# Layer 1: delta-x transposes of two groups right after delta x, first sum of y of each group one step on, 432 tokens of the C products on VectorE

## The chip, the cores and the metric

The kernel runs on one core of one Trainium2 chip. The metric is the device time of one execution in microseconds (us); the time before is the median of three runs. A profile of one execution shows the engines: PE (TensorE matmul; PEld is its weight load), DVE (VectorE), ACT (ScalarE), POOL (GpSimd) and SP (SyncE, which issues the DMAs).

## The reference

A batch of 32 images of 96 channels and 56x56 pixels goes through two layers. Layer 0 is an inverted-residual convolution block (1x1, depthwise 3x3, squeeze-excite, 1x1). Layer 1, which the change concerns, is two Mamba blocks in a row over the 3136 tokens of each image, then a 1x1 fusion and a batch norm. Cut to what matters, one Mamba block is:

```python
h  = layernorm(seq);  xs, z = split(h @ in_w)          # 96 -> 2 x 192
xc = silu(causal_conv4(xs) + conv_b)
dt, Bm, Cm = split(xc @ xproj_w)                        # 6, 16, 16
delta = softplus(dt @ dt_w + dt_b)                      # 192 channels
dA  = exp(delta[..., None] * A)                         # 192 x 16 states a token
dBx = delta[..., None] * Bm[:, :, None, :] * xc[..., None]
hstates = scan over tokens: h = dA * h + dBx
y   = einsum('blds,bls->bld', hstates, Cm) + Dp * xc
out = seq + (y * silu(z)) @ out_w
```

All arithmetic is float32.

## The kernel before, in words

Layer 1 works in chunks of 784 tokens: 32 images of 4 chunks, each through two blocks, so 256 chunks ("units" in the code). The chunks of the two blocks alternate. A chunk takes 24 steps, one scan each. There are three groups (k = 0, 1, 2) of 64 channels, and a group has eight steps in four pairs (j = 0 to 3, four of the 16 states each). A scan works on 128 partitions, 32 channels times four states, over 784 tokens.

What one step needs, with the names and lines that the profile uses:

- `da` (L1004, ACT): exp(delta * A). In the pair j = 0 of a group it goes to a lent buffer in SBUF, shown as `bx<-deltab`; in all other steps to a PSUM tile of the pool `dpool`, which has two buffers.
- `bx` (L1041, POOL): delta x times B, for a pair of steps at once, in the pairs j = 1 to 3.
- `bp` (L1018, PE, in `fill`): the same product for the pair j = 0, made by matmuls from `ut`, the transposed delta x of the group, and `diag`, a block-diagonal of B. It goes to a buffer of the same `dpool`, so the bp of step t can't begin before the scan of step t-2 is done. In a chunk these are steps 0, 1, 8, 9, 16 and 17; `fill(at + 1)` stands in the program one step ahead of its scan.
- `hh` (L1052, DVE): the scan itself.
- `hc`: hh times C for a pair of steps. The first LP tokens of each step are DVE's (L1060), from `cp`, a copy of C in PSUM that ACT makes (L1029); the other tokens are POOL's (L1068).
- `y`: ACT seeds the PSUM tile of a group with Dp * xc (L1086, `seed`); PE adds the sum over states of each pair to it (L1099, `reduce`); DVE multiplies the finished y by the gate z (L1110, `gated`). There is one PSUM buffer for y, so the seed of a group waits for the gate product of the group before.
- `state` (L1077, ACT): the last column of a pair's scans, kept for the next chunk of the image.

Between these stands the preparation of later chunks, a list of (time, function) pairs written out by hand in `prepare`. Time is counted in steps; step 0 is two chunks before the chunk's own first scan, so that its own steps are 48 to 71, and the steps 24 to 47 fall together with the 24 steps of the chunk before. Within a step the fraction sets the place: below 0.05 ahead of the step's seed and exp; 0.05 to 0.08 after bp and ahead of the sums of y; all others at the end. The functions that matter here, at the places in the chunk that is being scanned:

- step 2 to 5: `conv`, PE's matmuls of xs (L773) for the chunk after next, and `keep` copies them out as xc (L784, ACT); they use the banks of pool `pp`, two buffers which all small PE results share in the order in which they are asked for;
- steps 9 to 12: the output projection `o` (L905, L909), the gate projection `z` (L789) and the centering of a later chunk, `cen` (L702), whose squares ACT takes as `sx` (L707);
- step 14: `variance` (L712, var), 14 PE rows from both halves of sx; step 17: the root on ACT and three small Newton instructions on DVE (L729 to L734);
- steps 9 to 11: `input_u` (L864, POOL) makes delta x (`us`) of the three groups for the next chunk;
- `turn_u` (L848, PE) transposes the us of one group into a bank, and `keep_u` (L854 and L855, ACT) copies it to `ut`. Group 0 does this in steps 19 and 20 of the chunk before; groups 1 and 2 in steps 5 to 7 of their own chunk;
- step 7: the Softplus burst on ACT, and step 15 the Silu burst: a change of the activation table, one or two passes and a change back.

The order on each engine is that of the program (`tc.manual_schedule()`); only the semaphore waits decide when an instruction starts. The body of a step is in this order: inject, early preparation, seed, decay, bring, bursts, scan, gated, product, save, rest, fill, preparation from 0.05 to 0.08, reduce, preparation from 0.08, fetch (the DMAs).

Of the kernel before, what the change touches and what calls it, by code (L numbers as in the profile page):

```python
# [24 lines left out]
NL, NS, DIN, RANK, KC = 2, 16, 192, 6, 4  # L25
LC = 784
HB = LC // 2
LP = 416
NQ = L // LC
RB = HB // W  # L30
DG = 8
# [29 lines left out]
def conv_mamba_kernel(ctx, tc, a, out):  # L61
# [43 lines left out]
    with ExitStack() as ph:  # L105
# [119 lines left out]
        for i in range(NHB):  # L225
            t = hp3.tile([128, H + 2, W + 2], F32, name=f"hpad{i}", tag=f"hpad{i}")
# [303 lines left out]
    with ExitStack() as ph:  # L530
# [14 lines left out]
        def bank(name):  # L545
            return pp.tile([128, 512], F32, name=name, tag="p")

        def wt(shape, tag, bufs, n):
            return work.tile(shape, F32, name=f"{tag}_{n}", tag=tag, bufs=bufs)
# [132 lines left out]
        def cols(h):  # L682
            return slice(h * HB, h * HB + HB)

        def prepare(n):
# [14 lines left out]
            def center(h):  # L700
                ps = d["cen", h] = bank(f"cen_{n}_{h}")
                pe.matmul(ps[:C, :HB], cen, seqs[c, i][:, cols(h)], start=True, stop=True)  # L702

            def square(h):
                if h == 0:
                    d["sq"] = wt([128, LC], "sx", 1, n)[:C]
                s.activation(d["sq"][:, cols(h)], d["cen", h][:C, :HB], AF.Square)  # L707
# [17 lines left out]
            def newton(step):  # L725
                va, rs = d["va"], d["rs"]
                if step == 0:
                    d["nw"] = wt([TK, NK], "nw", 1, n)
                    v.scalar_tensor_tensor(d["nw"], rs, -0.5, va, ALU.mult, ALU.mult)  # L729
                if step == 1:  # L730
                    v.tensor_mul(d["nw"], d["nw"], rs)
                if step == 2:
                    to = wt([TK, NK], "rs", 1, n)
                    v.scalar_tensor_tensor(to, d["nw"], 1.5, rs, ALU.add, ALU.mult)  # L734
                    d["rs"] = to
                    if q == 0:
                        g.memset(xn[:, : KC - 1], 0.0)
# [40 lines left out]
            def keep(tag, bufs, ps, k):  # L778
                if k == 0:
                    d[tag] = wt([128, NB, HB], tag, bufs, n)  # L780
                if tag == "dl":
                    s.activation(d[tag][:, k, :], d[ps, k][:, :HB], AF.Identity, bias=dp[:, i, k, 0:1])
                else:
                    s.copy(d[tag][:, k, :], d[ps, k][:, :HB])  # L784
# [22 lines left out]
            def project_dt(k):  # L807
                ps = d["dtp", k] = bank(f"dt_{n}_{k}")
                for r in both:
                    pe.matmul(ps[r, :HB], wd[r, i, k, :], d["bcs"][r, :], start=True, stop=True)  # L810
# [34 lines left out]
            def turn_u(k):  # L845
                ps = d["utp", k] = bank(f"ut_{n}_{k}")
                for b in range(4):
                    pe.transpose(ps[: TSZ[b], b * 128 : b * 128 + 128], d["us"][:, k, TOFF[b] : TOFF[b] + TSZ[b]], eye)  # L848

            def keep_u(k):  # L850
                ut = d["ut", k] = wt([TB, 4, 2, 64], "ut", 3, f"{n}_{k}")
                ps = d["utp", k].rearrange("p (b h m) -> p b h m", b=4, h=2)
                z = TSZ[-1]
                s.copy(ut[:, 0], ps[:TB, 0])  # L854
                s.copy(ut[:z, 1:], ps[:z, 1:])  # L855
# [10 lines left out]

            steps = [(-20.5, load)]
            for h in range(2):
                steps += [((-11.9, -10.94)[h], lambda h=h: center(h)), ((-10.98, -9.99)[h], lambda h=h: square(h))]
            steps += [(-9.94, variance), (-7.9, root), *[(t, lambda m=m: newton(m)) for m, t in enumerate((-6.3, -6.2, -6.1))]]  # L870
            for m in range(2):
                steps += [((-6.7, -5.5)[m], lambda m=m: turn(m)), (-5.7 + m, lambda m=m: normalise(m))]
# [9 lines left out]
            steps += [(17.6, project_bc), (18.2, store_bc), (18.6, turn_b), (19.2, diagonal)]  # L882
            for k in range(NB):
                steps += [((20.6, 21.5, 21.6)[k], lambda k=k: project_dt(k)), ((21.2, 22.1, 22.2)[k], lambda k=k: keep("dl", 1, "dtp", k))]
                steps += [((43.5, 53.6, 54.3)[k], lambda k=k: turn_u(k)), ((44.1, 54.2, 55.01)[k], lambda k=k: keep_u(k))]
            for m in range(6):
                steps += [(26.9 + m, lambda m=m: scatter(*divmod(m, 3)))]
            steps += [(32.1, lambda: spread("delta", d["dl"], slice(0, NB)))]
# [54 lines left out]
        LAG = 4  # L943

        def place(t):
            k, r = divmod(t, 2 * SG)
            return k, r // 2, r % 2
# [38 lines left out]
        def by_pe(at):  # L986

            return place(at % NT)[1] == PEJ

        def lend(at):  # L990

            if by_pe(at) and at % 2 == 0:
                to = wt([128, 2, LC], "bx", 3, at)
                for p in range(2):
                    das[at + p] = to[:, p, :]
# [27 lines left out]
        def bring(at):  # L1023

            n, t = divmod(at, NT)
            k, j, p = place(t)
            if p == 1:
                cps[at] = cpool.tile([128, LP], F32, name=f"cp_{at}", tag="cp")
                s.copy(cps[at], data[n]["C", j][:, :LP])  # L1029

        def beside(x):

            return x.unsqueeze(1).to_broadcast([128, 2, x.shape[-1]])
# [23 lines left out]
        def product(at):  # L1057

            if place(at % NT)[2] == 1:
                v.tensor_mul(hcs[at - 1][:, :, :LP], hhs[at - 1][:, :, :LP], beside(cps.pop(at)))  # L1060

        def rest(at):
# [3 lines left out]
            if p == 1:  # L1066
                hcs[at - 1] = wt([128, 2, LC], "hc", 3, at)
                g.tensor_mul(hcs[at - 1][:, :, LP:], hhs[at - 1][:, :, LP:], beside(data[n]["C", j][:, LP:]))  # L1068

# [9 lines left out]
        def seed(at):  # L1079

            n, t = divmod(at, NT)
            k, j, p = place(t)
            if j == 0 and p == 1:
                i, d = units[n][1], data[n]
                yps[k] = ypool.tile([128, 512], F32, name=f"y_{n}_{k}", tag="y")
                s.activation(yps[k][:, :HB], d["xc"][:, k, :], AF.Copy, scale=dp[:, i, k, 1:2])  # L1086

        def reduce(at):

            n, t = divmod(at, NT)  # L1090
            i, d = units[n][1], data[n]
            k, j, p = place(t)
            if p == 0:
                return
            hc = hcs.pop(at - 1)
            for h in range(2):
                for p in range(2):
                    r0 = h * 64 + p * DB
                    pe.matmul(  # L1099
                        yps[k][r0 : r0 + DB, :HB], rel, hc[:, p, h * HB : h * HB + HB],  # L1100
                        start=False, stop=j == SG - 1, skip_group_check=True,
                    )
# [9 lines left out]
        total = len(units) * NT  # L1112
        todo, early = {}, {}
        for n in range(len(units)):
            steps, bursts = prepare(n)
# [9 lines left out]
        def ahead(at):  # L1125

            return (2, 1) if at % NT == 0 else (3, 2)
# [5 lines left out]
        with tc.manual_schedule():  # L1133
            for at in range(min(todo), max(todo) + 1):
                for m in (2, 3):
                    if 0 <= at + m < total and by_pe(at + m) and (at + m) % 2 == 0 and ahead(at + m)[0] == m:
                        lend(at + m)
                if 0 <= at + 4 < total:
                    inject(at + 4)
                for u, step in todo.get(at, ()):  # L1140
                    if u < 0.05:
                        step()
                if 0 <= at - LAG < total:
                    seed(at - LAG)
                if 0 <= at + 1 < total and not by_pe(at + 1):
                    decay(at + 1)
                for x in range(at, at + 5):
                    pair = x // 2 * 2
                    if 0 <= x < total and by_pe(x) and pair - ahead(pair)[x - pair] == at:
                        decay(x)  # L1150
                if 0 <= at < total:
                    bring(at)
                for step in early.get(at, ()):
                    step()
                if 0 <= at < total:
                    scan(at)
                if 0 <= at - LAG - 1 < total:
                    gated(at - LAG - 1)
                if 0 <= at - 1 < total:
                    product(at - 1)  # L1160
                if 0 <= at - 2 < total:
                    save(at - 2)
                if 0 <= at < total:
                    rest(at)
                if 0 <= at + 1 < total and by_pe(at + 1):
                    fill(at + 1)
                for u, step in todo.get(at, ()):
                    if 0.05 <= u < 0.08:
                        step()
                if 0 <= at - LAG < total:  # L1170
                    reduce(at - LAG)
                for u, step in todo.get(at, ()):
                    if u >= 0.08:
                        step()
                for t, tag in BEFORE[at % NT]:
                    fetch(at + t, (tag,))
# [79 lines left out]
```

## Time and profile before

| | |
|---|---|
| median of three runs | 18172.63 us (18170.29 to 18190.06) |
| profiled execution | 18204.1 us, of which 18202.3 us span |
| layer 1 | its first scan starts at 3055.5 us, its last at 17901.6 us |
| hh scans on DVE | 6144, 1774 to 1837 ns each |
| hc on DVE / on POOL | 3072 of 998 ns / 3072 of 1760 ns |
| bx on POOL | 2304 of 3542 ns |
| cp on ACT | 3072 of 513 ns |
| mean granted PE clock | 0.912 |

How to read it: PE, DVE, ACT and POOL are all busy for three quarters of the span or more, so what a change is worth is not read from shares but from the steps in which one engine waits for another. Busy time of PE counts matmuls that overlap. The granted clock is the share of its full clock that PE was given; a matmul's duration depends on it.

### The profile page before, as it was taken

To read this page: it belongs to the slowest core of one execution; us is meant where nothing else is said; L and a number is where in the kernel's file an instruction comes from. 1 tells how busy PE (TensorE), PEld (TensorE's weight loads), DVE (VectorE), ACT (ScalarE), POOL (GpSimd) and SP (SyncE) were. 2 spreads that over 40 slices of the span, in tenths; PEclk is the share of its full clock that TensorE was granted. 3 is DMA by queue.
4 is the path that set the end of the run, shared out by engine and by line. 5 is a ranking of instruction groups with operands and counts; after the bars stand their busy time and mean duration, and the time that the engine had idled before them with its cause. 6 is when DMAs were issued, how large, how long until landed. Compare 5 with 4: busy or idle time off the path is not lost.

```text
span 18202.3 us, 515600 instructions
## 1 busy us (share of the span) xinstructions
PE 15733.6 (86%) x212542; PEld 8423.4 (46%) x212542; DVE 16751.8 (92%) x12755; ACT 14204.1 (78%) x26476; POOL 14151.6 (78%) x6254
## 2 busy tenths in 40 slices
PE   9999998888888888888888888888888888888882
PEld 4444444444444444444444444444444444444441
DVE  9999996999999999999999999999999999999993
ACT  5555555888888888888888888888888888888884
POOL 0000002999999999999999999999999999999993
PEclk9999998999999999999999999999999999999996
DMA  1111113777777777777777777777777777777768
GB/s 35 29 29 29 29 29 88 182 183 183 182 185 186 184 183 183 183 183 186 184 183 182 183 182 186 184 184 183 183 183 184 186 183 182 184 182 182 186 182 220
DMA packets 1723533, 2893.14 MB, mean 159 GB/s; under 512 B 712886, under 2 KB 950670, under 8 KB 1714790
## 3 DMA queue, kind: packets, MB, share of 16 engines
q1 hardware_dynamic: 1712534, 2821.54, 59.6%
q0 software_dynamic: 6656, 38.54, 1.0%
q8 instruction: 1668, 27.33, 0.6%
q14 instruction: 691, 5.66, 0.1%
q10 hardware_dynamic: 1984, 0.07, 0.0%
HBM read 2402.42 MB, written 455.82 MB: 157 GB/s over the span
## 4 chain that ended last, share of the span: by engine, by line
PE 22%; ACT 16%; issue 12%; DMA 11%; DVE 9%; SPq 7%; POOL 5%; ACTq 0%; POOLq 0%; DVEq 0%
PE bp L1018 9%; DVE hh L1052 5%; ACT da L1004 5%; ACT bx L1004 4%; SPq L982 4%; DVE hc L1060 3%; DMA bdiag<-bt 3%; DMA deltab<-deltad 3%; PE y L1099 3%; SPq L969 3%; POOL hc L1068 2%; POOL bx L1041 2%; PE bc L798 2%; PE o L909 2%; DMA C<-bcd 2%
## 5 line engine op out<-in xcount | busy, mean ns | idle before, releaser
L1041 POOL TENSOR_TENSOR bx<-ub,B 128x1568 f32<-128x1568 f32 x2304 | 8160.7, 3542 | 16.2 <-DMA B<-bcd 16.2
L1052 DVE TENSOR_TENSOR_SCAN hh<-da,state,bx 128x784 f32<-128x784 f32 x3456 | 6257.5, 1835 | 53.1 <-ACT da L1004 50.2
L1068 POOL TENSOR_TENSOR hc<-hh,C 128x736 f32<-128x736 f32 x3072 | 5407.9, 1760 | 747.9 <-DVE hh L1052 476.0
L1004 ACT ACTIVATE da<-deltab,acol 128x784 f32<-128x784 f32 x4608 | 4253.4, 923 | 1192.4 <-DVE hh L1052 1184.8
L1099 PE MATMUL y<-hc,rel 128*32 128x392 f32 x24576 | 2888.8, 544 | 551.0 <-ACT y L1086 547.4
L1018 PEld LDWEIGHTS bp<-diag,ut 91*32 91x32 f32 (+1 forms) x98304 | 2873.9, 131 | 931.9 <-DVE hh L1052 544.1
L1018 PE MATMUL bp<-diag,ut 91*32 91x91 f32 (+1 forms) x98304 | 3192.1, 293 | 116.6 <-DVE hh L1052 100.7
L1060 DVE TENSOR_TENSOR hc<-hh,cp 128x832 f32<-128x832 f32 x3072 | 3065.6, 998 | 0.1
L1052 DVE TENSOR_TENSOR_SCAN hh<-bx,state,bp 128x784 f32<-128x784 f32 x1152 | 2116.7, 1837 | 491.3 <-PE bp L1018 488.6
masks.py:197 POOL MEMSET eye<- 128x128 f32 x2 | 0.4, 204 | 2923.3 <-ACT x L427 2923.0
L773 PE MATMUL xs<-xn,wx 97*64 97x392 f32 x12288 | 2250.3, 508 | 0.5 <-ACT xc L784 0.4
L1052 DVE TENSOR_TENSOR_SCAN hh<-da,bx 128x784 f32<-128x784 f32 x1152 | 2017.9, 1774 | 29.6 <-ACT da L1004 28.1
L340 DVE SCALAR_TENSOR_TENSOR h<-hpad,hp,h 128x1568 f32<-128x1568 f32 x1024 | 1895.3, 1851 | 33.2
L1029 ACT COPY cp<-C 128x416 f32<-128x416 f32 x3072 | 1576.4, 513 | 95.6 <-DVE hc L1060 93.3
L1004 ACT ACTIVATE bx<-deltab,acol 128x784 f32<-128x784 f32 x1536 | 1467.8, 956 | 0.0
L773 PEld LDWEIGHTS xs<-xn,wx 97*64 97x64 f32 x12288 | 816.5, 137 | 1357.4 <-issue 1264.4
L1099 PEld LDWEIGHTS y<-hc,rel 128*32 128x32 f32 x24576 | 623.9, 118 | 1523.9 <-ACT y L1086 1044.7
L307 PE MATMUL dw<-hpad,diag 32*32 32x392 f32 x36864 | 1124.8, 525 | 0.6 <-issue 0.4
L1052 DVE TENSOR_TENSOR_SCAN hh<-bx,bp 128x784 f32<-128x784 f32 x384 | 683.0, 1779 | 244.2 <-PE bp L1018 228.3
L245 PE MATMUL c<-x,w 96*128 96x392 f32 x2048 | 785.3, 526 | 118.2 <-ACT hpad L252 96.2
L848 PE MATMUL ut<-eye,us 128*91 128x128 f32 (+1 forms) x3072 | 582.3, 320 | 340.7 <-ACT xc L784 340.3
L307 PEld LDWEIGHTS dw<-hpad,diag 32*32 32x32 f32 x36864 | 680.8, 106 | 375.4 <-issue 132.0
(195 smaller groups left out, 20083.7 us busy)
## 6 DMA issues: line engine op xcount, KB each, us to landing
ub<-ud SPq DMA_DIRECT2D x3072, 196.0 KB
deltab<-deltad SPq DMA_DIRECT2D x3072, 196.0 KB
C<-bcd SPq DMA_DIRECT2D x4096, 98.0 KB
diag<-bdiag SPq DMA_DIRECT2D x1024, 294.8 KB
B<-bcd SPq DMA_DIRECT2D x3072, 98.0 KB
deltad<-dl SPq DMA_DIRECT2D x512, 294.0 KB
ud<-us SPq DMA_DIRECT2D x1536, 98.0 KB
x<-in_x_dram SPq DMA_DIRECT2D x32, 1176.0 KB
```

The lines of the kernel that those rows point to most:

```text
L245: pe.matmul(ps[:p, k, :HB], w1[:, ct * 128 : ct * 128 + p], xs[b][:, c0 : c0 + HB], start=True, stop=True)
L307: pe.matmul(ps[r][to : to + 32, :HB], diag[src, n, t, :], hb[src, r0 : r0 + RB, dx : dx + W], start=t == 0, stop=t == 8, skip_group_check= ...
L340: v.scalar_tensor_tensor(acc, src, tap, acc, ALU.mult, ALU.add)
L773: pe.matmul(d["xs", k][h * 64 : h * 64 + 64, :HB], wx[:, i, o, k * 64 : k * 64 + 64], xn[:, o + h * HB : o + h * HB + HB], start=o == 0, s ...
L1004: s.activation(das[at], d["delta", k][:, p, :], AF.Exp, scale=acol[:, j, i, 2 * k + p : 2 * k + p + 1])
L1018: pe.matmul(ps[sg * DB : sg * DB + DB, o : o + z], d["ut", k][:z, b, h, p * DB : p * DB + DB], dg[:z, sg // 2, h, x : x + z, sg % 2], star ...
L1029: s.copy(cps[at], data[n]["C", j][:, :LP])
L1041: g.tensor_mul(bx, data[n]["u", k], beside(data[n]["B", j]))
L1052: v.tensor_tensor_scan(hhs[at - p][:, p, :], das.pop(at), bxs.pop(at), state[i][:, t : t + 1] if c % NQ else 0.0, ALU.mult, ALU.add,)
L1060: v.tensor_mul(hcs[at - 1][:, :, :LP], hhs[at - 1][:, :, :LP], beside(cps.pop(at)))
L1068: g.tensor_mul(hcs[at - 1][:, :, LP:], hhs[at - 1][:, :, LP:], beside(data[n]["C", j][:, LP:]))
L1099: pe.matmul(yps[k][r0 : r0 + DB, :HB], rel, hc[:, p, h * HB : h * HB + HB], start=False, stop=j == SG - 1, skip_group_check=True,)
```

## The change

Three edits, all in layer 1.

1. `turn_u` and `keep_u` of groups 0 and 1 move to steps 13 to 15 of the chunk before, next to the centering and variance (transposes of group 0 and then of group 1 in steps 13 and 14, their copies at the head of steps 14 and 15). Group 2 takes the place that group 0 had, steps 19 and 20. Steps 5 to 7 have none any more. The second `center` moves by a hundredth, so that it comes after the transposes of group 0. The copies of group 0 stand ahead of the second sx on ACT, the transposes of group 1 ahead of var on PE.
2. The seed of y, and the first sum of y of each group (pair j = 0), are made one step later: the seed in steps 6, 14 and 22 and not 5, 13 and 21, and the first sum likewise. The other sums stay.
3. LP is 432 and not 416: DVE takes 16 more tokens of each step's C product, ACT copies 16 more to cp, POOL takes 16 fewer.

```diff
-LP = 416
+LP = 432
...
-                steps += [((-11.9, -10.94)[h], lambda h=h: center(h)), ((-10.98, -9.99)[h], lambda h=h: square(h))]
+                steps += [((-11.9, -10.93)[h], lambda h=h: center(h)), ((-10.98, -9.99)[h], lambda h=h: square(h))]
...
-                steps += [((43.5, 53.6, 54.3)[k], lambda k=k: turn_u(k)), ((44.1, 54.2, 55.01)[k], lambda k=k: keep_u(k))]
+                steps += [((37.06, 38.05, 43.5)[k], lambda k=k: turn_u(k)), ((38.005, 39.01, 44.1)[k], lambda k=k: keep_u(k))]
...
-                if 0 <= at - LAG < total:
-                    seed(at - LAG)
+                if 0 <= at - LAG - 1 < total:
+                    seed(at - LAG - 1)
...
-                if 0 <= at - LAG < total:
-                    reduce(at - LAG)
+                for t in (at - LAG - 1, at - LAG):
+                    if 0 <= t < total and by_pe(t) == (t == at - LAG - 1):
+                        reduce(t)
```

The order of the instructions on PE and ACT from the gate projection to step 17, as the program has it after the change:

```text
PE : z, z, y, z, cen(half 0), ut(group 0), cen(half 1), ut(group 1), var x14, y(first sum), bp(step 16), y, bp(step 17), y, ct, bc
ACT: z, sx(half 0), da, bx<-deltab, cp, ut(group 0) copies, sx(half 1), seed y, da, bx<-deltab, ut(group 1) copies, cp, Silu burst, root, da
```

## The prediction

> **What bounds the kernel now.** I read the busy times first, then the waits of VectorE (DVE), then one chunk of layer 1 in time order on DVE, PE and ACT, and last the granted clock by stretch.
>
> ```profile
> span 18202.3 us, 515600 instructions
> ...
> PE 15733.6 (86%) x212542; PEld 8423.4 (46%) x212542; DVE 16751.8 (92%) x12755; ACT 14204.1 (78%) x26476; POOL 14151.6 (78%) x6254
> ```
>
> DVE is nearest to full. Its waits in layer 1 have one main name, the products bp that PE makes for the two steps that open each group:
>
> ```profile
> DVE hh L1052 <- PE bp L1018: 716.9, 647, 2.3
> ...
> DVE hh L1052 <- ACT da L1004: 78.3, 249, 1.0
> ```
>
> Layer 1 has 256 chunks of 24 steps, so 716.9 us is 2.8 us a chunk. I take chunk 96, whose first scan starts at 8623.42; "+x" is us after that. On DVE (start, duration, line, idle before and releaser), the scans of steps 7, 8, 16, 17 and 18:
>
> ```profile
> 8639.79 1.84 DVE L1052 TENSOR_TENSOR_SCAN hh<-da,state,bx 128x784 f32<-128x784 f32 x1
> 8643.90 1.84 DVE L1052 TENSOR_TENSOR_SCAN hh<-bx,state,bp 128x784 f32<-128x784 f32 x1 [2.28 <-PE bp L1018]
> ...
> 8662.05 1.82 DVE L1052 TENSOR_TENSOR_SCAN hh<-bx,state,bp 128x784 f32<-128x784 f32 x1
> ...
> 8664.95 1.85 DVE L1052 TENSOR_TENSOR_SCAN hh<-bx,state,bp 128x784 f32<-128x784 f32 x1 [0.17 <-PE bp L1018]
> ...
> 8667.58 1.85 DVE L1052 TENSOR_TENSOR_SCAN hh<-da,state,bx 128x784 f32<-128x784 f32 x1 [0.33 <-ACT da L1004]
> ```
>
> Step 8 carries most (over chunks 4 to 251, scans counted in order, its mean is 1.95 us; steps 16 to 18 have 1.06 together). PE ahead of step 8, and ahead of step 16:
>
> ```profile
> 8635.20 0.86 PE L1099 MATMUL y<-hc,rel 128*32 128x392 f32 x8 [1.64 <-ACT y L1086]
> 8636.00 2.06 PE L773 MATMUL xs<-xn,wx 97*64 97x392 f32 x8
> 8637.98 1.11 PE L848 MATMUL ut<-eye,us 128*120 128x128 f32 x4
> 8639.88 1.11 PE L848 MATMUL ut<-eye,us 128*120 128x128 f32 x4 [0.79 <-ACT xc L784]
> 8640.92 2.85 PE L1018 MATMUL bp<-diag,ut 120*32 120x120 f32 x64
> ...
> 8655.71 0.87 PE L1099 MATMUL y<-hc,rel 128*32 128x392 f32 x8 [0.56 <-ACT y L1086]
> 8656.50 0.75 PE L712 MATMUL var<-mean,sx 96*112 96x1 f32 x6
> 8658.33 0.95 PE L712 MATMUL var<-mean,sx 96*112 96x1 f32 x8 [1.08 <-ACT sx L707]
> 8659.51 1.92 PE L1018 MATMUL bp<-diag,ut 120*32 120x120 f32 x64 [0.24 <-DVE hh L1052]
> ```
>
> The first y waits for ACT, the transposes wait for a bank, and only then does bp start. The clock by stretch (stretch, length, busy of PE, PEld, DVE, ACT, POOL, then PEclk):
>
> ```profile
> 8636.90:8643.70 6.80, 6.01 (x80) 4.27 (x80) 4.73 (x4) 6.11 (x13) 6.27 (x3) 0.50 0.97 230
> 8643.70:8660.80 17.10, 15.23 (x202) 7.56 (x198) 16.90 (x13) 14.76 (x26) 16.44 (x10) 1.00 0.42 99
> 8660.80:8664.20 3.40, 3.40 (x70) 2.51 (x63) 3.40 (x3) 3.37 (x4) 3.40 (x2) 0.50 1.01 280
> ```
>
> PE runs at half clock through the bp of step 8 and the second half of that of step 16. Sorting the trace by clock, one step's bp takes 1.62 us at full and 2.78 at half, a y sum 0.80 and 1.31, a group's transposes 0.58 and 1.11.
>
> **The change, part by part.**
>
> *Step 8.* Both transposes and the y sum leave PE's step 5. After the 28 xs rows PE is free at +11.7. ACT no longer holds y behind the end of the gate product: scan 4 ends at +10.65, then da 0.84, bx 0.84, cp 0.44, state 0.09, xc 0.38 and y 0.59 by their rows: +13.85; PE's sum ends at +14.7. bp then waits for the buffer of scan 6 (ends 8638.95) and starts at +15.6, not +17.50. Scan 8 could start at +18.27 by DVE, so the 2.28 us fall to 0 or 0.1. For step 9 I need bp, y, bp: in full clock they end at +19.9 (the second waits for scan 7), in half clock at +22.5; by the 5.06 us that they take now, at +20.7. PE is idle for 3.1 of the 3.9 us before +15.6, more than now, so I take +21.0; scan 9 starts at +21.1, before at +23.16: **2.1 us won** so far.
>
> *Steps 9 to 16.* From that bp to the first sx, PE and ACT run the same work back to back (8.86 us now, 8645.98 to 8654.84): sx ends at +29.85. ACT then takes da, bx, cp and state (2.21), the new ut copies (0.54, as from 8641.02 to the next copy at 8641.56) and the second sx (0.48): +33.05. Behind the copies on ACT stand sx, y, da, bx, the second copies and the Silu burst. The projection banks are two, so the second transposes wait for the first copies: +32.6, then 0.58 to 1.11. POOL's us for them ends at +32.33 now, and earlier once its wait for scan 9 (0.66) shrinks. var then does all its 14 rows in a row, 1.63 (today six of them fill the wait for sx): +34.8 to +35.3. The y sum, which now stands before the wait, comes after var: 0.80 to 1.31, to +35.6 to +36.65. Then bp, 1.62 to 2.78: **+37.25 to +39.4**; today it ends at +38.01. So about two of the won microseconds are owed here: 0.6 to 1.1 of transposes, 0.6 of var, 0.8 to 1.3 of y.
>
> *Which clock.* From about +30.8 to +35 PE has only transposes, var and idle time, less than today, when a y sum stood in it and a half-clock stretch still followed. I take half clock up to the end of this bp (+39.4), full after.
>
> [...]
>
> *Steps 16 to 18.* Scan 16 starts at +39.45 (DVE alone: +36.6). y and bp at full end at +41.85; scan 16 and its product take 2.70, so scan 17 starts at +42.15, and scan 18, after 1.75 and the three small Newton instructions with their gaps (0.65), at +44.55. Now it is +44.16: **0.39 later**. ACT's own path there (second sx, then 9.8 us of y, da, bx, ut copies, cp, burst, root and da) ends at +42.85 and is hidden.
>
> *432 tokens.* The gate product (392 elements, 534 ns) and hc (832, 998 ns) give 1.05 ns an element; 32 more are 34 ns, 12 times a chunk. If nothing hid them it is 105 us; nine of twelve are in the sums above, the last three add **0.10**. POOL loses 32 elements of 2.14 ns (from 832 more of them costing 1782 ns between bx and hc), 69 ns each: 212 us less, all of it beside DVE: no wait of DVE names POOL. ACT's cp grows by at most 27 ns (513 less 473 for 24 elements): inside waits. No moved step issues a DMA; SP's order stands.
>
> *Sum.* 0.39 + 0.10 = 0.49 us a chunk, times 256: 125 us. Against its own execution (18204.1, of which 18202.3 span) that is 18329; the median of the runs is 31.5 lower, so 18298. Bounds of the unknown clock: full clock throughout (below), and half through the bp of step 17 too, which ends at +43.5: scan 18 at +45.95, 1.9 a chunk, 18659.
>
> **Rivals.**
>
> *Faster:* PE keeps its full clock at steps 14 to 17. Then bp ends at +37.25, scan 17 starts at +40.05 and scan 18 is set by ACT at +42.9: 1.26 less, 1.16 with the products, 297 us: **17876**. For it: half of today's bp (743 of the 1490 in the steady part) run wholly at full clock. Against: the quiet stretch. It decides from 0.5 us on, that is once half of one bp's half-clock surcharge (1.16) falls away.
>
> *No change:* a chunk now lasts 58.0 us on average, and a half-clock stretch lies at the same offset of chunks 48 apart: each of the windows +37.4 to +40.7 of chunks 48, 96, 144, 192 and 240 has PEclk 0.50, and the next 3.3 us 0.99 or 1.00. So the chunk keeps step with the gate's own beat (17 stretches of 3.41 are 58.0). If the new chunk's length crosses that value for some offset, it settles there: **18173**. The sum, 58.5, is near, but no row shows how far the pull reaches.
>
> *Slower still:* half clock in both bp pairs, 18659 at most.
>
> **How the numbers follow.** Forecast, with its heavier half: 0.50 (0.38 within 18230 to 18420). No change: 0.17. Faster: 0.33. The range leaves out the heaviest of the slow cases and reaches to the fast rival: 17870 to 18480. 0.2% (36 us) is about what a measurement can tell; the same cases give 0.33, 0.17, 0.50.
>
> **What would show it.** Right: scan 8's wait is gone, that of step 16 is 2 us or more, var comes as 14 rows directly ahead of y and bp, PEclk is 0.50 there. Wrong: step 16's wait stays under 1 us (the clock, or the bank's wait shorter than I count), or step 8 still waits for bp (half clock over its rows), or DVE waits for ACT da at step 18 (ACT's copies bind).

## The result, and the profile after

The changed kernel takes 18562.75 us (median of six runs, 18552.18 to 18570.98); the kernel before, run beside it, takes 18177.89. The ratio is 1.021 with the interval 1.02 to 1.0221: **385 us slower**, 1.5 us for each of the 256 chunks. The forecast had the direction and the place, but a third of the size (125 us), and its range ended at 18480.

The page of the profiled execution of the changed kernel (busy time and share of the span by engine):

```profile
span 18556.8 us, 516623 instructions
...
PE 15893.6 (86%) x212542; PEld 8666.2 (47%) x212542; DVE 16874.8 (91%) x12755; ACT 14251.2 (77%) x26476; POOL 13953.0 (75%) x6254
```

PE has the same 212542 matmuls, and they take 160 us more; the mean clock is 0.890 where it was 0.912. DVE has 123 us more work, 108 of it the longer hc. The waits that bear on the prediction (who waits for whom: total us, times, the longest):

```profile
DVE hh L1052 <- PE bp L1018: 878.1, 717, 15.3
...
PE ut L848 <- POOL hc L1068: 274.2, 147, 1.9
...
DVE hh L1052 <- ACT da L1004: 117.0, 249, 1.8
...
DVE hh L1052 <- POOL bx L1041: 37.1, 38, 1.0
```

DVE's wait for bp, which the change goes for at step 8, has grown from 716.9 to 878.1 us (one wait of 15.3 of them is the start of layer 1). The second line, PE's wait at the transposes, is not there at all before; what it waits for is not POOL, as the rows of chunk 96 show below.

Chunk 96 again, whose first scan now starts at 8741.42; "+x" is counted from there. DVE in time order: the scans of steps 7, 8 and 9, then those of 16, 17, 18 and 20.

```profile
8757.95 1.84 DVE L1052 TENSOR_TENSOR_SCAN hh<-da,state,bx 128x784 f32<-128x784 f32 x1
8760.12 1.85 DVE L1052 TENSOR_TENSOR_SCAN hh<-bx,state,bp 128x784 f32<-128x784 f32 x1 [0.33 <-PE bp L1018]
...
8763.91 1.85 DVE L1052 TENSOR_TENSOR_SCAN hh<-bx,state,bp 128x784 f32<-128x784 f32 x1 [1.00 <-PE bp L1018]
...
8781.38 1.85 DVE L1052 TENSOR_TENSOR_SCAN hh<-bx,state,bp 128x784 f32<-128x784 f32 x1 [1.81 <-PE bp L1018]
...
8784.09 1.84 DVE L1052 TENSOR_TENSOR_SCAN hh<-bx,state,bp 128x784 f32<-128x784 f32 x1
...
8786.29 1.85 DVE L1052 TENSOR_TENSOR_SCAN hh<-da,state,bx 128x784 f32<-128x784 f32 x1
...
8791.09 1.85 DVE L1052 TENSOR_TENSOR_SCAN hh<-da,state,bx 128x784 f32<-128x784 f32 x1 [0.24 <-ACT da L1004]
```

The 2.28 us ahead of step 8 have become 0.33; 1.00 has appeared ahead of step 9 and 1.81 ahead of step 16. PE in the same chunk, at the two pairs of bp:

```profile
8755.44 0.87 PE L1099 MATMUL y<-hc,rel 128*32 128x392 f32 x8 [2.41 <-ACT y L1086]
8757.14 2.85 PE L1018 MATMUL bp<-diag,ut 120*32 120x120 f32 x64 [0.83 <-DVE hh L1052]
8759.76 1.53 PE L1099 MATMUL y<-hc,rel 128*32 128x392 f32 x8
8761.07 2.76 PE L1018 MATMUL bp<-diag,ut 120*32 120x120 f32 x64
...
8775.54 0.62 PE L848 MATMUL ut<-eye,us 128*120 128x128 f32 x4 [1.90 <-POOL hc L1068]
8776.00 1.51 PE L712 MATMUL var<-mean,sx 96*112 96x1 f32 x14
8777.44 1.53 PE L1099 MATMUL y<-hc,rel 128*32 128x392 f32 x8
8778.75 2.50 PE L1018 MATMUL bp<-diag,ut 120*32 120x120 f32 x64
8781.06 0.84 PE L1099 MATMUL y<-hc,rel 128*32 128x392 f32 x8
```

No transposes stand ahead of the first pair any more, yet bp, y, bp run at the slow durations (2.85, 1.53, 2.76), after PE had been idle for 2.41 and 0.83 us. The second stretch is the predicted one: transposes after a wait, var as 14 rows in a row, then y and bp at the slow durations. What ended PE's wait of 1.90 us is not POOL's hc that the profile names. These rows lie ahead of its end, at 8775.54:

```profile
8772.02 1.02 POOL L864 TENSOR_TENSOR us<-dl,xc 128x392 f32<-128x392 f32 x1
8772.99 1.67 POOL L1068 TENSOR_TENSOR hc<-hh,C 128x704 f32<-128x704 f32 x1
...
8774.97 0.47 ACT L855 COPY ut<-ut 91x384 f32<-91x384 f32 x1
```

POOL's us of group 1 had ended at 8773.04 and its hc at 8774.66, while ACT's copy of group 0 ended at 8775.44, 0.10 us before the transposes of group 1 start. It is the same in the chunks 4 to 251: they start 0.10 us after that copy, and in the median 2.2 us after us is ready.

The granted clock is 0.50 in both slow stretches (stretch, length, busy of PE, PEld, DVE, ACT, POOL, PEclk, then the DMA share and GB/s):

```profile
8756.80:8763.60 6.80, 6.46 (x136) 5.47 (x136) 5.78 (x5) 6.21 (x9) 6.80 (x4) 0.50 0.68 160
8763.60:8777.30 13.70, 11.69 (x80) 5.19 (x70) 13.39 (x10) 10.71 (x23) 13.70 (x9) 1.00 0.36 92
8777.30:8780.70 3.40, 3.40 (x58) 2.44 (x61) 2.27 (x2) 3.37 (x6) 3.40 (x1) 0.50 0.99 274
```

One chunk is an example, so I counted the idle time of DVE ahead of each step's scan over the chunks 4 to 251, from the scans in order (mean us a chunk; for 17 and 18, and for 20 and 21, the two together):

| step | before | after |
|---|---|---|
| 8 | 1.95 | 0.31 |
| 9 | 0.01 | 0.49 |
| 16 | 0.58 | 2.52 |
| 17 and 18 | 0.48 | 0.11 |
| 20 and 21 | 0.21 | 0.55 |
| 0 | 0.00 | 0.27 |
| all | 3.23 | 4.25 |

Waits grew by 1.02 us; the tokens add 12 times 35 ns, 0.42; the sum nearly fills the growth of the chunk from 58.03 to 59.53. PE ran 13.7 us of each chunk at half clock, before 9.9.

### The profile page after: what moved, and what is told of

It reads as the page before. It is cut to its first block, busy times and chain, and to the rows that moved or that the text cites. A ratio compares the mean times of both kernels' runs of the same rounds, so it can differ in the third digit from the quotient of the medians.

```text
span 18556.8 us, 516623 instructions
## 1 busy us (share of the span) xinstructions
PE 15893.6 (86%) x212542; PEld 8666.2 (47%) x212542; DVE 16874.8 (91%) x12755; ACT 14251.2 (77%) x26476; POOL 13953.0 (75%) x6254
## 4 chain that ended last, share of the span: by engine, by line
PE 21%; issue 21%; DVE 17%; ACT 11%; POOL 10%; DMA 2%; SPq 2%; ACTq 0%; DVEq 0%; POOLq 0%
DVE hh L1052 10%; DVE hc L1060 6%; PE bp L1018 6%; POOL bx L1041 4%; POOL hc L1068 4%; PE y L1099 4%; PE bc L798 3%; ACT da L1004 2%; POOL us L864 2%; PE var L712 2%; ACT bx L1004 1%; SPq L982 1%; ACT sx_t L751 1%; PE dt L810 1%; PE z L789 1%
## 5 line engine op out<-in xcount | busy, mean ns | idle before, releaser
L1068 POOL TENSOR_TENSOR hc<-hh,C 128x704 f32<-128x704 f32 x3072 | 5206.5, 1695 | 1326.7 <-DVE hh L1052 722.6
L1099 PE MATMUL y<-hc,rel 128*32 128x392 f32 x24576 | 3102.6, 580 | 648.7 <-ACT y L1086 497.5
L1018 PEld LDWEIGHTS bp<-diag,ut 91*32 91x32 f32 (+1 forms) x98304 | 3035.8, 135 | 1316.0 <-issue 627.6
L1018 PE MATMUL bp<-diag,ut 91*32 91x91 f32 (+1 forms) x98304 | 3255.4, 298 | 208.3 <-DVE hh L1052 207.8
L1060 DVE TENSOR_TENSOR hc<-hh,cp 128x864 f32<-128x864 f32 x3072 | 3173.2, 1033 | 0.1
L773 PE MATMUL xs<-xn,wx 97*64 97x392 f32 x12288 | 2141.1, 497 | 0.4 <-ACT xc L784 0.4
L1029 ACT COPY cp<-C 128x432 f32<-128x432 f32 x3072 | 1615.6, 526 | 149.7 <-DVE hc L1060 135.9
L848 PE MATMUL ut<-eye,us 128*91 128x128 f32 (+1 forms) x3072 | 537.5, 302 | 480.3 <-POOL hc L1068 274.2
L798 PE MATMUL bc<-xc,wbc 64*64 64x392 f32 x3072 | 615.3, 534 | 329.7 <-DVE rs L734 320.4
```

Of the source, the lines that this page charges most:

```text
L773: pe.matmul(d["xs", k][h * 64 : h * 64 + 64, :HB], wx[:, i, o, k * 64 : k * 64 + 64], xn[:, o + h * HB : o + h * HB + HB], start=o == 0, s ...
L798: pe.matmul(ps[r, :HB], wbc[r, i, k], d["xc"][r, k, :], start=k == 0, stop=k == NB - 1)
L1018: pe.matmul(ps[sg * DB : sg * DB + DB, o : o + z], d["ut", k][:z, b, h, p * DB : p * DB + DB], dg[:z, sg // 2, h, x : x + z, sg % 2], star ...
L1099: pe.matmul(yps[k][r0 : r0 + DB, :HB], rel, hc[:, p, h * HB : h * HB + HB], start=False, stop=j == SG - 1, skip_group_check=True,)
```

## The experiments

Each ratio is against the kernel before, run beside it, with its 95% interval; microseconds "less" or "more" than another kernel are differences of the medians. Idle matmuls are added work: no later instruction reads what they write.

**The three parts alone.**

```diff
-LP = 416
+LP = 432
```

> Only the 432 tokens; transposes and sums of y stay as before. Theory A (the loss is PE's row ahead of step 16: copies of group 0, transposes of group 1, var, first sum of y, bp, mostly at half clock): 12 products a chunk of 34 ns more on VectorE, partly beside its waits for bp: 0 to 105 us slower than before, the waits of steps 8 and 16 as before. Rival B (the tokens on the fullest engine are the loss): 105 us or more, up to the whole 385.

Measured: 18182.82, ratio 1.0001 (0.9992 to 1.0011). The added DVE work, some 105 us, costs nothing that can be measured. The scans in layer 1, from the lines of the kernel before and then of this one (count, duration in ns as least, median and most, first and last start):

```profile
L1052 DVE TENSOR_TENSOR_SCAN hh<-da,state,bx x3456: 1814/1840/1853, 3115.7 to 17901.6; 128x784 f32<-128x784 f32 x192
...
L1052 DVE TENSOR_TENSOR_SCAN hh<-bx,bp x384: 1755/1785/1790, 3055.5 to 17715.8; 128x784 f32<-128x784 f32 x192
```

```profile
L1052 DVE TENSOR_TENSOR_SCAN hh<-da,state,bx x3456: 1817/1841/1852, 3086.8 to 17872.2; 128x784 f32<-128x784 f32 x192
...
L1052 DVE TENSOR_TENSOR_SCAN hh<-bx,bp x384: 1757/1781/1789, 3026.5 to 17685.1; 128x784 f32<-128x784 f32 x192
```

Layer 1's first scan is the first start of the second line, its last the last start of the first. There are 6143 steps between them: 17901.6 less 3055.5, over 6143 and times 24, is 58.00 us a chunk; 17872.2 less 3026.5 gives 58.00 as well. The trace of the kernel before has 1128 stretches of one granted clock, and all of them start on a grid of 3.4133 us, to 1 ns; 17 of its intervals are 58.03 us. This grid is the "gate's own beat" of the "no change" rival, and the chunk is as long as that rival said: the added work came out of the waits, and DVE's idle time ahead of scans fell from 3.23 to 2.87 us a chunk.

```diff
-                if 0 <= at - LAG < total:
-                    seed(at - LAG)
+                if 0 <= at - LAG - 1 < total:
+                    seed(at - LAG - 1)
...
-                if 0 <= at - LAG < total:
-                    reduce(at - LAG)
+                for t in (at - LAG - 1, at - LAG):
+                    if 0 <= t < total and by_pe(t) == (t == at - LAG - 1):
+                        reduce(t)
```

> Only the seed and the first sum of y of each group a step later; transposes and 416 tokens as before. Theory A: the sum of group 1 leaves the gap in which PE waits for sx and stands behind var, 0.8 to 1.5 us ahead of bp of step 16, while the wait of step 8 stays: 100 to 300 us slower than before. Rival C (the sums have no part; the moved transposes are the loss): within 60 us of before.

Measured: 18297.47, ratio 1.0066 (1.0049 to 1.0082), 120 us slower. Step 8 keeps 1.73 us of its wait, since the transposes still stand there; step 16 rises to 0.93, step 0 to 0.18, and steps 20 and 21 to 0.55. The late sums alone are a loss.

```diff
-((43.5, 53.6, 54.3)[k], lambda k=k: turn_u(k)), ((44.1, 54.2, 55.01)[k], lambda k=k: keep_u(k))
+((37.06, 38.05, 43.5)[k], lambda k=k: turn_u(k)), ((38.005, 39.01, 44.1)[k], lambda k=k: keep_u(k))
```

(With it goes the second centering, from -10.94 to -10.93.)

> Only the transposes and their copies moved; sums of y and 416 tokens as before. Theory A: the wait of step 8 (1.95 us) goes, the sum of group 1 stays in the gap ahead of var, so bp of step 16 is late by the copies and the transposes alone (about 1 us less than in the changed kernel): 100 us faster to 150 us slower than before. Rival C (the moved transposes are the loss): 250 to 400 us slower.

Measured: 18043.4, ratio 0.9925 (0.9911 to 0.994), 134 us faster, where at most 100 was expected. Step 8's wait is gone with the transposes alone (0.06); step 16 has 1.79 us. So the move of the sums is not needed for step 8.

```diff
 (the changed kernel, with)
-LP = 432
+LP = 416
```

> The changed kernel with 416 tokens again. Theory A: 0 to 105 us faster than the changed kernel, so 280 to 385 us slower than before, the wait of step 16 still 2 us or more. Rival B (tokens): within 100 us of before.

Measured: 18393.34, ratio 1.0119 (1.0103 to 1.0134), 169 us less than the changed kernel, where 105 was the most that the tokens' own time allows. Step 16 has 2.47 us. Set against the transposes alone, the late sums raise step 16 by 0.68 us: the y sum now stands between var and bp. The three parts alone sum to 6 + 120 - 134 = -8 us, together they measure +385: the parts don't add.

**The last group's late sum.** The prediction put a price on the late sum of groups 0 and 1 only. That of group 2 moves too, from step 21 to step 22, where it stands directly ahead of the first bp of the next chunk. In the changed kernel, at the end of chunk 96:

```profile
8797.40 0.86 PE L1099 MATMUL y<-hc,rel 128*32 128x392 f32 x8
8798.08 1.66 PE L1018 MATMUL bp<-diag,ut 120*32 120x120 f32 x64
```

Here group 2 keeps its old place, all else is the changed kernel:

```diff
-                if 0 <= at - LAG - 1 < total:
-                    seed(at - LAG - 1)
+                for t in (at - LAG - 1, at - LAG):
+                    if 0 <= t < total and (place(t % NT)[0] < 2) == (t == at - LAG - 1):
+                        seed(t)
...
-                    if 0 <= t < total and by_pe(t) == (t == at - LAG - 1):
+                    if 0 <= t < total and (by_pe(t) and place(t % NT)[0] < 2) == (t == at - LAG - 1):
```

> The changed kernel, but seed and first sum of the last group at their old place (steps 21), those of groups 0 and 1 late. Theory A (the changed kernel loses in two places: about 2 us of wait at step 16, and 0.8 us after step 18, where the last group's late sum stands ahead of the bp of the next chunk and the quiet stretch ahead of it brings a third half-clock stretch): 100 to 200 us faster than the changed kernel, the waits of steps 20 and 0 as in the kernel before. Rival D (what is late after step 18 follows from step 16 alone): within 40 us of the changed kernel.

Measured: 18406.2, ratio 1.0122 (1.0107 to 1.0137), 157 us less than the changed kernel. The wait ahead of step 0 is gone (0.27 to 0.00), which makes step 23 0.30 shorter, the idle time ahead of steps 20 and 21 falls from 0.55 to 0.35, and the stretch from scan 18 to the next chunk's first scan is 14.23 us instead of 14.73. The half clock falls from 13.7 to 11.8 us a chunk. So of the 0.78 us that this stretch had grown, 0.50 go with group 2's late sum; of the 0.28 left, 0.14 are the wait of steps 20 and 21 (0.35 against 0.21 before) and 0.10 the longer products.

But the late sum is not the cause by itself. With 416 tokens and this sum still late (the run before this one), the stretch is 14.24 us: undoing either edit takes some 0.50 away (with the tokens, 0.10 of it is their own work). Of the parts alone, it is 14.54 with the late sums, 14.31 with the transposes and 13.89 with the tokens, against 13.95 before. PE's half clock in this stretch is 0.12 us a chunk before, 2.59 in the changed kernel, 0.81 here and 0.67 with 416 tokens; with the late sums alone it is 1.95, with the transposes alone 2.09.

**Is it the clock?** The kernel before, with 18 idle matmuls of bp's shape put between the two halves of var, into columns of its bank that nobody reads:

```diff
+                    if k == 2:
+                        for m in range(18):
+                            pe.matmul(
+                                ps[m % 4 * DB : m % 4 * DB + DB, HB : HB + TB], rel, eye[:, :TB],
+                                start=True, stop=True, skip_group_check=True,
+                            )
```

> The kernel before with 18 idle matmuls of bp's shape (about 0.9 us at full clock, to columns that nobody reads) between the two parts of var, where PE waits 1.08 us for sx. More work on PE and nothing else. Clock theory (the quiet stretch ahead of step 16 is what puts its bp at half clock): the clock stays at 1.0 there, the waits of steps 16 to 18 (1.06 us a chunk) fall to 0.4 or less, and the kernel is up to 170 us faster, or no faster where the chunk keeps step with the gate's beat. Rival (the clock there has another cause): same clock, waits as before or 0.2 us longer, same time or up to 50 us slower.

Measured: 18033.39, ratio 0.9922 (0.9904 to 0.994): 149 us less, by adding work. PE at step 16 of one chunk, and the clock of the stretch around it:

```profile
8565.46 0.75 PE L712 MATMUL var<-mean,sx 96*112 96x1 f32 x6
8566.14 1.22 PE L715 MATMUL var<-eye,rel 128*32 128x120 f32 x36
8567.29 0.95 PE L712 MATMUL var<-mean,sx 96*112 96x1 f32 x8
8568.47 1.66 PE L1024 MATMUL bp<-diag,ut 120*32 120x120 f32 x64 [0.24 <-DVE hh L1058]
```

```profile
8562.00:8574.00 12.00, 10.84 (x216) 6.97 (x213) 12.00 (x10) 11.15 (x16) 12.00 (x7) 1.00 0.56 148
```

The 1.08 us in which PE waited for the second sx are filled, the clock stays at 1.00 and bp takes 1.66. Over all chunks the half clock falls from 9.9 to 5.8 us, step 16's wait from 0.58 to 0.00, and step 8's from 1.95 to 0.82. What is late next is ACT:

```profile
DVE hh L1058 <- ACT da L1010: 357.3, 480, 2.5
...
DVE hh L1058 <- PE bp L1024: 263.2, 302, 15.4
```

The same in the changed kernel: 24 idle matmuls after the second centering, in the place where PE waits 1.90 us for the copies of group 0:

```diff
 (the changed kernel, in center, with)
+                    if h == 1:
+                        for m in range(24):
+                            pe.matmul(
+                                ps[m % 4 * DB : m % 4 * DB + DB, HB : HB + TB], rel, eye[:, :TB],
+                                start=True, stop=True, skip_group_check=True,
+                            )
```

> The changed kernel with 24 idle matmuls of bp's shape (some 1.2 us at full clock, to columns that nobody reads) right after the second centering, where PE then waits 1.9 us for the copies of group 0. Clock theory (of the 2.5 us wait at step 16 more than half is half clock over var, y and bp): var back from 2.4 to 1.3, y from 1.5 to 0.8, bp from 2.85 to 1.66 in most chunks, the wait of step 16 under 1.2 us, 200 to 500 us faster than the changed kernel. Rival (the row of work alone is the loss): within 60 us of the changed kernel.

Measured: 18181.56, ratio 0.9999 (0.9989 to 1.0008). **This one edit takes back 381 of the 385 us**, with every part of the change in place. PE at step 16, and its clock:

```profile
8645.63 1.44 PE L705 MATMUL cen<-eye,rel 128*32 128x120 f32 x48
8647.60 0.62 PE L854 MATMUL ut<-eye,us 128*120 128x128 f32 x4 [0.53 <-issue]
8648.06 1.45 PE L718 MATMUL var<-mean,sx 96*112 96x1 f32 x14
8649.43 0.87 PE L1105 MATMUL y<-hc,rel 128*32 128x392 f32 x8
8650.12 1.68 PE L1024 MATMUL bp<-diag,ut 120*32 120x120 f32 x64
```

```profile
8635.40:8662.70 27.30, 24.11 (x333) 13.73 (x326) 25.73 (x21) 23.70 (x52) 27.30 (x13) 1.00 0.64 166
```

The order of PE's instructions is that of the changed kernel; y takes 0.87 instead of 1.53, and bp 1.68 instead of 2.50. The mean wait at step 16 is 0.32 instead of 2.52, those at steps 17 and 18 are 0.72 together instead of 0.11, and steps 8 and 9 are as they were (0.34 and 0.53). The half clock is 9.8 us a chunk instead of 13.7. Over the chunks scan 18 starts at +43.41, before at +44.08 and in the changed kernel at +44.80, while the stretch behind it stays long (14.62 us, 13.95 before): the edit makes up for that part of the loss and does not remove it. The chunk is once more 58.01 us long, next to 17 intervals of the clock's grid (58.03). So the figure may be held there, and by itself the edit may be worth more; no run shows that.

**Groups moved singly.** First all three at a distance, in steps 13, 19 and 21 of the chunk before (the changed kernel has 13, 14 and 19), with the second centering at -10.93, without the late sums and with 416:

```diff
-((43.5, 53.6, 54.3)[k], lambda k=k: turn_u(k)), ((44.1, 54.2, 55.01)[k], lambda k=k: keep_u(k))
+((37.06, 43.5, 45.2)[k], lambda k=k: turn_u(k)), ((38.005, 44.1, 45.95)[k], lambda k=k: keep_u(k))
```

> The kernel before with the transposes spread: group 0 in step 13, group 1 in step 19 where group 0 had been, group 2 in step 21; sums of y and 416 tokens as before. Theory A: nothing is left ahead of bp of step 8, and var waits for the copies of group 0 only, not for a second transpose: the wait of step 8 under 0.3, that of step 16 under 1.2 us: 150 to 400 us faster than before. Rival C (moved transposes cost what they save wherever they stand): within 100 us of before.

Measured: 17832.79, ratio 0.9804 (0.979 to 0.9819). Step 8 has 0.03 us of wait, step 16 only 0.98; 6.0 us of half clock a chunk.

Then the same with the 18 idle matmuls in var:

> The spread transposes and the 18 idle matmuls of bp's shape between the parts of var. Clock theory: bp of step 16 at full clock, another 50 to 200 us faster than the spread kernel alone. Rival (the clock has another cause): the same or up to 100 us slower than it.

Measured: 18374.99, ratio 1.0106 (1.0091 to 1.0121): 542 us slower than without them, a clear miss. PE at step 16:

```profile
8711.54 0.75 PE L712 MATMUL var<-mean,sx 96*112 96x1 f32 x6 [1.90 <-ACT ut L861]
8712.22 1.39 PE L715 MATMUL var<-eye,rel 128*32 128x120 f32 x36
8713.55 1.66 PE L712 MATMUL var<-mean,sx 96*112 96x1 f32 x8
8715.13 2.85 PE L1024 MATMUL bp<-diag,ut 120*32 120x120 f32 x64
```

Here PE waits ahead of var, for ACT's copies, not within it. The idle matmuls come after that wait and lie on the path, and what follows them is slow all the same: the last 8 rows of var take 1.66 us and bp 2.85, where they took 0.95 and 1.66 with the same matmuls in the kernel before. They add their time and save nothing: the mean wait of step 16 is 3.01 us where it was 0.98.

Last, group 1 alone is moved, to step 21 of the chunk before; groups 0 and 2, the sums, the centering and 416 stay:

```diff
-((43.5, 53.6, 54.3)[k], lambda k=k: turn_u(k)), ((44.1, 54.2, 55.01)[k], lambda k=k: keep_u(k))
+((43.5, 45.2, 54.3)[k], lambda k=k: turn_u(k)), ((44.1, 45.95, 55.01)[k], lambda k=k: keep_u(k))
```

> The kernel before with one group's transposes moved: group 1 from step 5 of its own chunk to step 21 of the chunk before; groups 0 and 2, sums and tokens as before. Theory A: PE does the transposes of group 2 while bp of step 8 waits for the buffer of scan 6 anyway, so the wait of step 8 falls from 1.95 to under 0.5 us, and nothing is put ahead of step 16, whose wait stays at 0.5 to 1: 250 to 450 us faster than before, as the spread kernel or better. Rival E (both transposes must leave: the bank of the last one is free too late): the wait of step 8 over 1 us, less than 250 us faster.

Measured: **17647.97, ratio 0.9705 (0.9691 to 0.972)**, 536 us faster than the kernel before, more than the 450 expected, and the best of all. One wait of DVE, and PE ahead of step 8:

```profile
DVE hh L1052 <- PE bp L1018: 166.6, 338, 1.1
```

```profile
8413.39 0.65 PE L848 MATMUL ut<-eye,us 128*120 128x128 f32 x4 [0.28 <-ACT xc L784]
8414.59 1.70 PE L1018 MATMUL bp<-diag,ut 120*32 120x120 f32 x64 [0.54 <-DVE hh L1052]
```

The transposes of group 2 still stand ahead of bp and hurt nothing: bp is held by scan 6's buffer and not by them, and it runs at its full-clock duration (1.70). Step 8's mean wait is 0.00, step 16 keeps its old order (0.36), and the chunk is 55.89 us.

Two additions to it. With the 18 idle matmuls in var:

> The same with the 18 idle matmuls between the parts of var, in the gap in which PE waits for sx. Clock theory: bp of steps 16 and 17 at full clock, 50 to 200 us faster than the one-group kernel alone, the rest of the wait going over to ACT's da at steps 18 and 20. Rival: the same or slower.

Measured: 17782.17, ratio 0.9778 (0.9763 to 0.9792), 134 us slower than without them, another miss. Step 16's wait is gone (0.01), as meant, but DVE now waits for ACT's exp where it waited 67.9 us before:

```profile
DVE hh L1058 <- ACT da L1010: 292.5, 540, 1.7
```

and in many chunks the half clock lies 42 to 53 us into the chunk instead. Why it goes there is left open.

With 432 tokens:

> The one-group kernel with 432 tokens, where no beat of the clock holds the chunk (its chunks take 55.9 us) and POOL's waits for scans have shrunk from 476 to 61 us in all. Theory A (VectorE, 95% busy, sets the chunk): 12 products a chunk of 34 ns more, 60 to 105 us slower than the one-group kernel. Rival F (POOL is now as late as VectorE, and 69 ns less of it a product counts): the same or up to 100 us faster.

Measured: 17712.68, ratio 0.9747 (0.9731 to 0.9763), 65 us slower than with 416. The chunk grows from 55.89 to 56.15, 0.26 of the 0.42 that is added to DVE; half of the rest comes out of the waits (1.08 to 1.00 us a chunk).

## Why the prediction was right and wrong

**Right.** Slower, and through the mechanism named: step 8's wait goes (1.95 to 0.31), step 16's comes (0.58 to 2.52, "2 us or more"), with var as 14 rows ahead of y and bp, and these two at half clock: in chunk 96 PE was busy for 1.76 of the 3.41 us from 8773.89 on, and the next stretch, from 8777.30 on, has 0.50. That the clock carries the loss at step 16 is shown by the idle matmuls in the changed kernel (0.9999): with the same order, the path from the second transposes to scan 16 shrinks by 2.2 us. The order has its part in it. Between scans 9 and 18 the kernel before is at half clock for nearly as long (5.41 us a chunk, 5.57 after), with a wait of only 0.58 us at step 16; the change puts more of the path to bp into that time. And with idle matmuls in both kernels the changed one is still 148 us behind (18181.56 against 18033.39). In chunk 96 the parts up to the first bp hold: y's sum starts at +14.02 (the seed's end predicted at +13.85), bp at +15.72 (+15.6), the second sx 3.15 us after the first (3.20), and ACT is not what holds scan 18.

**Steps 8 and 9: too good.** The term "I take +21.0" for the second bp lay between two clocks. In chunk 96 it ended at +22.41, by the half-clock end (+22.5), and scan 9 started at +22.49 instead of +21.1. PE was busy for only 0.87 of the 3.41 us ahead of 8756.80, and the clock was 0.50 from there on; I had weighed that idle time and still taken a value nearer to full clock. Over the chunks scan 9 gains 0.93 us (22.70 to 21.77 on the mean), not 2.1.

**Steps 9 to 18: two errors that partly met.** The second transposes came 1.5 us later than I put them (+34.12 against +32.6). Of this, 1.4 us is the late second bp, which the row of work on ACT carries on; the wait itself is the one that I named, for the copies of group 0, and POOL's us was ready before. But the half clock began only at +35.9 in this chunk, within var, so that transposes, var, y and bp took 5.71 us from there and not the 6.83 of my slow end: the first bp ended at +39.83, scan 16 started at +39.96, scan 18 at +44.87, against +39.4, +39.45 and +44.55. Over the chunks scan 18 is 0.73 us later than before, not 0.39: 0.34 times 256, 87 us.

**After step 18: the term that failed.** I gave 0.10 us, three longer products, with PE at full clock. It is 0.78, with 2.59 us of half clock a chunk (0.12 before): from scan 18 to the next chunk 14.73 us instead of 13.95. The difference, 0.68 times 256, is 173 us. I had followed the late sums of groups 0 and 1 and left out that group 2's moves too, from step 21 to step 22, directly ahead of the next chunk's first bp. Putting it back took 157 us off. But it is not the cause by itself: with the tokens taken back and this sum still late the stretch is 14.24 us. How the parts together delay DVE there was not traced to one wait, and stays open: ahead of step 0 DVE waits 0.15 us for POOL's bx, 0.07 for ACT's sx and 0.04 for bp. With the 87 these 173 are 260 us, the gap between 125 and 385.

**The tokens' price.** "Nine of twelve are in the sums" and 34 ns each was a count of work. Measured, the same 16 tokens cost 6 us in the kernel before (none, by its interval), 65 with group 1 moved alone, and 169 in the changed kernel. In the first the chunk kept its 58.00 us. In the third they make the chunk 0.79 us longer, and 0.48 of it lies behind scan 18; why they are so dear there, no run isolates. POOL's relief came as counted (199 us less busy, predicted 212) and brought nothing; a wait of DVE for POOL's bx, of which I had said that there is none, is new with 37.1 us.

**The rivals.** *No change:* it fits the runs in that three kernels with different work hold 58.0 us a chunk, next to 17 intervals of the clock's grid (58.03); no run shows what holds them there. But the changed kernel was too far beyond it: it lies at 59.5. *Faster* needed full clock at steps 14 to 17; the changed kernel without idle matmuls has 5.57 us of half clock a chunk between scans 9 and 18. *Slower still* (18659) was nearest in size, and in chunk 96 the first pair of bp does run at half clock throughout; but the second bp of the other pair takes 1.66 us, full clock, and two thirds of what I missed lies behind step 18, where this rival has nothing.

What the traces show of the clock: the 1128 stretches of one granted clock in the kernel before and the 1328 in the changed one all start on a grid of 3.4133 us. I sorted the grid's intervals at full clock by what PE did in them (from chunk 4 on). Where PE was busy for less than half of an interval, all 12 in the kernel before and all 471 in the changed one were followed by half clock; where it was busy for 80% or more, none of 2300 and none of 2155. Idle matmuls of 1.22 and 1.44 us in the gap ahead of step 16 left the clock at 1.00 in the two chunks shown. The transposes I had counted with the idle time, and that does not fit. Over the ten kernels without idle matmuls, where other matmuls filled 30 to 50% of an interval and there were no transposes (of us or xn), 648 of 659 intervals were followed by half clock (43 of 43 in the kernel before and the changed one); where transposes filled another 30% or more, none of 991 was (none of 143 in these two). This sorts traces and is no experiment, but by it PE's idle time, and not its transposes, makes the stretch ahead of step 16 quiet.

## What to carry to other kernels

When a step is moved out of one wait, look at what the new place does to PE's clock: a wait on PE costs its own length and can then cost the slower work behind it as well (in chunk 96 of the changed kernel, waits of 2.41 and 0.83 us were followed by a clock of 0.50 and a bp of 2.85 us, which takes 1.66 at full clock). Moving the least that clears the wait (one group's transposes, 0.9705) was worth far more than moving everything (1.021). And when a helper is shifted by one step for "each group", follow every group to its new place, above all the one whose new place lies directly ahead of the next loop turn's first products.

## What the runs showed that I had not expected

- Useless matmuls can pay. In the kernel before, 18 of them took 149 us off; in the changed kernel 24 took off 381. Behind the wait (spread kernel) they cost 542 us, and with group 1 alone moved 134, although there they filled it.
- Three kernels with different work have the same chunk. The kernel before, the one with 432 tokens and the changed one with idle matmuls run at 58.00, 58.00 and 58.01 us a chunk, next to 17 intervals of the clock's grid of 3.4133 us (58.03). Some 105 us of tokens did not show there; in chunks of other lengths (55.89 and 58.71 us without them) the same tokens cost 65 and 169.
- Three parts measured alone gave +6, +120 and -134 us, and together +385. The wait that the sums and the transposes make jointly ahead of step 16 is in neither alone to that extent (0.93, 1.79, and together 2.47 us with 416 tokens).
